# Graph attention in three layers: where vector instructions that build one-hot rows stand among the copies of gathered rows

## The chip, the cores and the metric

The kernel runs on one core of a Trainium2 chip. Five engines work side by side, each on its own instruction queue: TensorE (PE, with its weight loads shown as PEld), VectorE (DVE), ScalarE (ACT), GpSimd (POOL) and SyncE (SP, which only issues transfers here). The metric is the device time of one execution in microseconds (us), lower is better; a comparison uses the median of several runs.

## The reference

Three layers of a graph transformer over 6250 nodes of 64 values and 206250 directed edges, which are sorted by their target node. For each edge a score is formed from the target's query and the source's key plus an edge term; a softmax over the edges of each target weighs the sources' values, which are summed:

```python
q = x @ Wq + bq
kj = (x @ Wk + bk)[src] + edge_attr @ We
alpha = jnp.sum(q[dst] * kj, axis=-1) / jnp.sqrt(D)
p = jnp.exp(alpha - segment_max(alpha, dst)[dst])
w = p / segment_sum(p, dst)[dst]
agg = segment_sum((v[src] + e) * w[:, None], dst)
x = agg + x @ Ws + bs
```

ReLU follows each layer and a layer norm the first two; behind the third stand a log-softmax, the sum with the input and a last norm.

## The kernel before

The sorted edges are cut into chunks of 768 (six tiles of 128). Four chunks are a **unit**; a layer has 67 full units and a rest. The rows `x[src]` of a unit are its 24 tiles `feat`. They come in two ways.

**Gathered.** For most tiles GpSimd issues an indirect transfer of 128 rows (`gather`, line 610). Each chunk's gathers wait for a copied index tile `gate` (ScalarE, line 642), which `release` writes two units ahead of use; four `feat` buffers are in turn.

**Picked.** In layers 1 and 2 twelve tiles of a unit (three in each of its four chunks) are not gathered but picked by TensorE out of the node table `parts`, which lies in SBUF. So twelve gathers a unit are left. A pick multiplies a one-hot `hot` by parts of the table (line 1453) into the PSUM tile `ps_x`, which then holds, for each wanted row, four candidates side by side. VectorE takes the first with a copy (line 1408) and lays the other three over it under the mask `which` with three predicated copies (line 1410). The one-hot comes from `keys`, numbers that an SP transfer brings in (line 1913): for each tile depth `t` two comparisons with a constant (line 1382, 128 partitions by 512). Three depths make six such instructions for a unit; the mask `which` (line 1371) is one instruction more.

The class `Picker` drives this. `plan` gives three depths for each of two pairs of chunks; `picks` makes four steps of a unit from that: pair 0 with depths 0 and 1, pair 0 with depth 2, pair 1 with depths 0 and 1, pair 1 with depth 2. I call them the first to the fourth pick. One is made in each quarter `j` of a unit's loop, for the unit after it. `aim` hands a free one-hot buffer (there are four) to the next depth whose keys are `ready` and issues the mask and the comparisons. A buffer becomes free when the last pair that reads it has been multiplied, so two in the third pick and one in the fourth. `ready` is renewed at a unit's end, and there all six comparisons for the coming unit are issued in a row. `evacuate` issues the copies of a pick, `swap` three small ScalarE copies behind each pair.

All engines have their order fixed by the program's order (manual schedule), so an instruction that waits holds up what stands behind it on its engine.

A quarter of unit u also turns one chunk's rows with PE transposes (line 1754), which need that chunk's gathers, and ScalarE copies the result out (line 1757). In the second quarter, behind the second pick, VectorE forms the second half of the masked scores and their maximum for the unit before (lines 1781 and 1794); ScalarE's exponential follows (line 1800), and at the end of the third quarter PE transposes its result (line 1814). The weighted sums are line 1826.

In the first layer the sorting of the edges runs on VectorE and TensorE as well, and one-hots and copies are woven into it.

Of the kernel before, what the change touches and what calls it, by code (L numbers as in the profile page):

```python
# [17 lines left out]
ALU = mybir.AluOpType  # L18
# [22 lines left out]
KB = 4  # L41
# [11 lines left out]
NH = WB // KB  # L53
# [379 lines left out]
def main_path(  # L433
# [53 lines left out]
    nc = tc.nc  # L487
# [46 lines left out]
    def ps(use):  # L534
        tag = bank_of.get(use, use)
        wide = 2 if len(psum) > 1 and tag == "x" else 1
        return psum[-1].tile(
            [P, wide * 512], F32, tag=tag, name=f"ps_{tag}", bufs={"a": 2, "x": 2}.get(tag, 1)
        )
# [7 lines left out]
    def placed(layer, k):  # L547

        return k < NT and (layer > 0 or k >= U0)
# [105 lines left out]
    rank = const.tile([P, NH], F32, name="rank")  # L655
# [691 lines left out]
    class Picker:  # L1347


        def __init__(self, layer):  # L1350
            self.layer = layer
            self.room = 4 if layer else 2
            self.plan = {k: depth(picked(layer, k)) for k in range(len(batches)) if picked(layer, k)}
            self.todo = [(k, t) for k in self.plan for t in range(self.plan[k][0])]
            self.free = list(range(self.room))
            self.hots = {}
            self.which = {}
            self.quarter = 0
            self.swaps = []
            self.late = []  # L1360
            self.ready = set(keys)

        def aim(self):

            while self.free and self.todo and (self.layer, self.todo[0][0]) in self.ready:
                k, t = self.todo.pop(0)
                n = 2 * sum(t < most for most in self.plan[k]) * P
                if k not in self.which:
                    m = NP * LB
                    which = small.tile([P, m, KB], F32, name="which", bufs=2)  # L1370
                    nc.vector.tensor_tensor(
                        which,
                        kbs[:, k].rearrange("p v c -> p (v c)").unsqueeze(2).to_broadcast([P, m, KB]),
                        four[:, :KB].unsqueeze(1).to_broadcast([P, m, KB]),
                        ALU.is_equal,
                    )
                    self.which[k] = which
                at = self.free.pop(0)
                hot = stock[0].tile([P, NH, LB * P], F32R, name=f"hot{at}", bufs=1)[:, :, :n]
                first = t * LB * P  # L1380
                for h in range(NH):
                    nc.vector.tensor_scalar(  # L1382
                        hot[:, h], keys[self.layer, k][:, first : first + n], rank[:, h : h + 1], None, ALU.is_equal
                    )
                self.hots[k, t] = at, hot

        def swap(self, left=0):

# [8 lines left out]
        def evacuate(self):  # L1397

            if not self.late:
                return  # L1400
            k, pair, t, m, px, which = self.late.pop()
            found = loaded[self.layer, k][:, 2 * pair : 2 * pair + 2, t : t + m, 0]
            which = which.rearrange("p (t c) b -> p c t b", c=LB)[:, 2 * pair : 2 * pair + 2, t : t + m]
            px = px.rearrange("p t c b d -> p c t b d")

            def choose(b):
                if not b:
                    nc.vector.tensor_copy(found, px[:, :, :, 0])  # L1408
                    return
                nc.vector.copy_predicated(  # L1410
                    found,
                    which[:, :, :, b].bitcast(I32).unsqueeze(3).to_broadcast([P, 2, m, D]),
                    px[:, :, :, b],
                )
                if b == KB - 1 and t + m == self.plan[k][pair]:
                    self.swaps.append((k, pair, t + m))

            woven.extend((pair, partial(choose, b)) for b in range(KB))
            if self.layer or len(opened) > 1:
                weave(KB)  # L1420

        def flush(self):
# [14 lines left out]
        def batch(self, k):  # L1437

            for pair, t0, m in self.picks(k):
# [3 lines left out]
                self.aim()  # L1443
                bank = "x" if self.layer else "pssp"[self.quarter]
                px = ps(bank)[:, : m * 512].rearrange("p (t c b d) -> p t c b d", t=m, c=2, b=KB)
                for t in range(t0, t0 + m):
                    at, hot = self.hots[k, t]
                    for v in range(2):
# [12 lines left out]
                        self.free.append(self.hots.pop((k, t))[0])  # L1461
                self.late.append((k, pair, t0, m, px, self.which[k]))
                if self.layer:
                    due = len(self.swaps)
                    self.evacuate()
                    self.swap(len(self.swaps) - due)
                self.aim()
                yield
# [520 lines left out]
    for layer in range(L):  # L1989
# [8 lines left out]
        for u in range(NU - 2):  # L1998
# [10 lines left out]
            for j in range(LB):  # L2009
# [14 lines left out]
                    line.weights(u - 1, 1)  # L2024
                if j == 1:
                    line.begun()
                    if not layer and placed(0, u + 1):
                        line.most(u - 1, 1)
                        line.powers(u - 1)
# [39 lines left out]
                picker.flush()  # L2069
            picker.ready.update(keys)  # L2070
            picker.aim()
            for k in range(u + 2, u + 4):
                decode(layer, k)

# [134 lines left out]
```

## Time and profile before

| | |
|---|---|
| time, median of 3 runs | 4135.28 us (4134.92 to 4141.25) |
| the profiled execution | 4139.31 us, its span 4137.5 us |
| mean granted TensorE clock | 0.933 |
| busy, share of the span | PE 81%, PEld 58%, DVE 72%, ACT 57%, POOL 68% |
| gathers of layer 0 / of layers 1 and 2 | 1100 (`feat<-in_x`) / 1592 (`feat<-x,gate`) and 48 (`feat<-x,src_b`) |

In a group's row the columns are line, engine, operation, tiles, count, then busy us and mean ns of one, then the idle time of the engine just before these instructions and what ended it. A row of the timeline has start, duration, engine, line, operation, tiles, count of merged neighbours, and in brackets the idle time before. "issue" means that the engine waited for nothing that the profile shows.

### The profile page before, as it was taken

What the parts mean: (1) busy time and instruction counts of PE and PEld (TensorE: products, weight loads), DVE (VectorE), ACT (ScalarE), POOL (GpSimd) and SP (SyncE); (2) the same over time, 40 slices, a digit from 0 to 9 for tenths busy, and PEclk for the clock granted to TensorE, in tenths of its full rate; (3) what the DMA queues carried; (4) which work ended last, traced back from release to release, by engine and by line L of the source; (5) the groups of instructions that cost most, each with busy time, mean ns of one, the idle gap of its engine ahead of it and who ended that gap; (6) DMA issues with size and microseconds to landing.
All of it is one profiled execution on the core that took longest, in us unless ns stands there. A gap on an engine that the chain in (4) does not pass through costs nothing.

```text
span 4137.5 us, 105363 instructions
## 1 busy us (share of the span) xinstructions
PE 3364.6 (81%) x34183; PEld 2391.6 (58%) x34183; DVE 2977.8 (72%) x10306; ACT 2351.6 (57%) x6011; POOL 2827.9 (68%) x2774
## 2 busy tenths in 40 slices
PE   3889899999989899984778788888757878778776
PEld 1445555555555555553666666666646666666664
DVE  5677888888878888864667777777646667777775
ACT  0455565565656555563556556565635656666665
POOL 5467666666667666663777777777657777777774
PEclk9899999999999999996999999999969999999998
DMA  5667677666767666765677777777657677777774
GB/s 111 185 175 198 171 192 181 180 183 184 188 161 193 179 180 175 183 174 125 173 183 193 186 183 185 188 189 188 164 135 183 173 190 182 187 189 183 186 184 102
DMA packets 787997, 728.88 MB, mean 176 GB/s; under 512 B 487336, under 2 KB 612450, under 8 KB 787440
## 3 DMA queue, kind: packets, MB, share of 16 engines
q1 hardware_dynamic: 630436, 504.14, 47.6%
q0 software_dynamic: 88448, 90.75, 11.6%
q10 hardware_dynamic: 68556, 127.16, 8.7%
q8 instruction: 278, 4.55, 0.5%
q14 instruction: 279, 2.29, 0.2%
HBM read 562.78 MB, written 158.81 MB: 174 GB/s over the span
## 4 chain that ended last, share of the span: by engine, by line


## 5 line engine op out<-in xcount | busy, mean ns | idle before, releaser
L610 POOL DMA_INDIRECT feat<-x,gate x1592 | 1579.9, 992 | 485.4 <-issue 372.9
L610 POOL DMA_INDIRECT feat<-in_x,gate x1100 | 1175.4, 1069 | 652.6 <-ACT gate L642 323.5
L1453 PE MATMUL ps_x<-parts,hot 128*128 128x256 f32 x6336 | 941.8, 301 | 0.0
L1453 PEld LDWEIGHTS ps_x<-parts,hot 128*128 128x128 f32 x6336 | 841.8, 202 | 81.8 <-DVE feat L1410 62.5
L1757 ACT COPY featT<-ps_a 64x384 f32<-64x384 f32 x1320 | 627.1, 475 | 393.5 <-PE ps_a L1754 369.5
L1410 DVE COPY_PREDICATED feat<-which,ps_x 128x256 f32<-128x256 int32 (+1 forms) x1584 | 592.4, 374 | 54.3
L1408 DVE COPY feat<-ps_x 128x256 f32<-128x256 f32 (+1 forms) x528 | 187.7, 355 | 587.0 <-PE ps_x L1453 577.2
L1754 PE MATMUL ps_a<-ident,feat 128*128 128x128 f32 x2380 | 451.0, 289 | 176.2 <-DMA feat<-x,gate 139.7
L1101 DVE TENSOR_SCALAR hit<-ruler,pos 128x384 bf16<-128x384 f16 x1608 | 501.8, 324 | 30.3 <-PE ps_m L1121 30.2
L1754 PEld LDWEIGHTS ps_a<-ident,feat 128*128 128x128 f32 x2380 | 283.3, 144 | 385.7 <-issue 276.0
L1382 DVE TENSOR_SCALAR hot<-keys,rank 128x512 fp32r<-128x512 f16 (+1 forms) x1040 | 432.9, 482 | 9.1 <-DMA keys<-keyS 5.2
L1826 PE MATMUL ps_p<-feat,probT 128*32 128x128 f32 x6600 | 236.3, 295 | 91.4 <-ACT probT L1817 77.8
L1112 PE MATMUL ps_x<-hit,raw 128*64 128x384 bf16 x1608 | 293.8, 360 | 2.5 <-DVE hit L1101 2.2
L1112 PE MATMUL ps_x<-hit,rest 128*64 128x384 bf16 x1608 | 275.0, 338 | 0.0
L1112 PE MATMUL ps_x<-hit,end 128*64 128x384 bf16 x1608 | 274.2, 337 | 0.0
L1826 PEld LDWEIGHTS ps_p<-feat,probT 128*32 128x32 f32 x6600 | 193.6, 119 | 129.4 <-ACT probT L1817 102.9
L1767 PE MATMUL ps_s<-featT,q 128*32 128x384 f32 x1866 | 228.0, 496 | 11.6 <-DMA featT<-eaS 7.3
L1814 PE MATMUL ps_s<-ident,prob 128*128 128x128 f32 (+1 forms) x417 | 81.3, 307 | 191.6 <-ACT prob L1800 188.7
L1453 PE MATMUL ps_p<-parts,hot 128*128 128x256 f32 x992 | 163.8, 311 | 80.5 <-DVE feat L1410 73.5
L1800 ACT ACTIVATE prob<-prob,part 128x768 f32<-128x768 f32 x204 | 190.0, 931 | 68.7 <-DVE part L1794 60.1
L1453 PEld LDWEIGHTS ps_p<-parts,hot 128*128 128x128 f32 x992 | 137.1, 204 | 112.5 <-DVE feat L1410 91.8
L1833 ACT COPY part<-ps_p 128x128 f32<-128x128 f32 (+1 forms) x140 | 37.3, 267 | 244.9 <-PE ps_p L1826 239.8
(281 smaller groups left out, 5960.6 us busy)
## 6 DMA issues: line engine op xcount, KB each, us to landing
featT<-eaS SPq DMA_DIRECT2D x658, 192.0 KB
feat<-eaP SPq DMA_DIRECT2D x134, 768.0 KB
raw<-in_ea SPq DMA_DIRECT2D x536, 96.0 KB
eaS<-eT ACTq DMA_DIRECT2D x134, 384.0 KB
keys<-keyS SPq DMA_DIRECT2D x132, 384.0 KB
eaP<-feat ACTq DMA_DIRECT2D x128, 384.0 KB
shade<-maskS SPq DMA_DIRECT2D x198, 192.0 KB
fourth<-eaS SPq DMA_DIRECT2D x134, 192.0 KB
```

Source lines behind the costliest of these rows:

```text
L610: nc.gpsimd.indirect_dma_start(out=feat[:, c, t, 0], out_offset=None, in_=xts[layer][:, :], in_offset=bass.IndirectOffsetOnAxis(ap=index[: ...
L1101: nc.vector.tensor_scalar(hit, ruler, self.pos[:, at : at + 1], None, ALU.is_equal)
L1112: nc.tensor.matmul(self.px[j * D : (j + 1) * D, :HE], self.parts[2 * h + i].thirds[part][:, j, t * D : (t + 1) * D], self.hits[h, 2 * i + ...
L1382: nc.vector.tensor_scalar(hot[:, h], keys[self.layer, k][:, first : first + n], rank[:, h : h + 1], None, ALU.is_equal)
L1408: nc.vector.tensor_copy(found, px[:, :, :, 0])
L1410: nc.vector.copy_predicated(found, which[:, :, :, b].bitcast(I32).unsqueeze(3).to_broadcast([P, 2, m, D]), px[:, :, :, b],)
L1453: nc.tensor.matmul(px[:, t - t0, v].rearrange("p b d -> p (b d)"), hot[:, h, (2 * pair + v) * P : (2 * pair + v + 1) * P], those[:, i, b0 ...
L1754: nc.tensor.transpose(pt[:, t * P : (t + 1) * P], rows[:, 2 * t * D : 2 * (t + 1) * D], ident)
L1757: nc.scalar.copy(featT[:, :, h, :], pt[h * D : (h + 1) * D, : n * P].rearrange("d (i e) -> d i e", e=P))
L1767: nc.tensor.matmul(p_s[rows, :w], self.q[:, rows], self.featT[j][:, cols], start=True, stop=True)
L1800: nc.scalar.activation(self.prob[:n, : self.cols], self.prob[:n, : self.cols], AF.Exp, bias=neg, accum_out=self.part[:n, P + 1 : P + 2],)
L1826: nc.tensor.matmul(p_g[rows, :].rearrange("n (h d) -> n h d", h=2), self.probT[:, t, rows], batch[:, j, t], start=(t == 0), stop=(t == sel ...
```

## The change

In layers 1 and 2 `aim` no longer issues the two comparisons of a depth; it puts them on a list `cuts`. `cut` issues the oldest of the list. `evacuate` issues a pick's four copies and one listed comparison behind each; `batch` calls `aim` once more before `evacuate`, so that buffers which the pick has just freed are handed on at once, and issues what is left of the list behind the copies. `cut_for` issues, ahead of a pick's products, those of its own one-hots that still stand on the list. The keys count as ready in the second quarter instead of at the unit's end. Layer 0 keeps its order.

```diff
@@ aim
+                those = keys[self.layer, k][:, first : first + n]
                 for h in range(NH):
-                    nc.vector.tensor_scalar(
-                        hot[:, h], keys[self.layer, k][:, first : first + n], rank[:, h : h + 1], None, ALU.is_equal
+                    self.cuts.append(
+                        partial(nc.vector.tensor_scalar, hot[:, h], those, rank[:, h : h + 1], None, ALU.is_equal)
                     )
                 self.hots[k, t] = at, hot
+                if not self.layer:
+                    self.cut(NH)
+
+        def cut(self, n=1):
+
+            while n and self.cuts:
+                self.cuts.popleft()()
+                n -= 1
+
+        def cut_for(self, *those):
+
+            last = max(i for i, at in enumerate(self.hots) if at in those)
+            self.cut(max(0, len(self.cuts) - NH * (len(self.hots) - 1 - last)))
@@ evacuate
+            if self.layer:
+                for b in range(KB):
+                    choose(b)
+                    self.cut()
+                return
             woven.extend((pair, partial(choose, b)) for b in range(KB))
-            if self.layer or len(opened) > 1:
+            if len(opened) > 1:
                 weave(KB)
@@ batch
+                self.cut_for(*((k, t) for t in range(t0, t0 + m)))
...
                 if self.layer:
+                    self.aim()
                     due = len(self.swaps)
                     self.evacuate()
+                    self.cut(len(self.cuts))
                     self.swap(len(self.swaps) - due)
@@ the loop over a unit's quarters
                 if j == 1:
                     line.begun()
+                    if layer:
+                        picker.ready.update(keys)
...
             picker.ready.update(keys)
             picker.aim()
+            picker.cut(len(picker.cuts))
```

Only VectorE's order differs; the other four engines have the same instructions in the same order. (Lines above 1354 are numbered higher in the changed file: the comparisons are line 1394 there, the copies 1423 and 1425, the mask 1372.)

VectorE at the end of a unit in layer 2 and in the first quarter of the next, before: the third pick's copies (two depths wide), the fourth's (one depth wide), the mask, six comparisons, the first half of the masked scores, the first pick's copies.

```order
L1408 COPY feat<-ps_x 128x2x128
L1410 COPY_PREDICATED feat<-which,ps_x 128x2x128 x3
L1408 COPY feat<-ps_x 128x2x64
L1410 COPY_PREDICATED feat<-which,ps_x 128x2x64 x3
L1371 TENSOR_TENSOR which<-kbs,four 128x64
L1382 TENSOR_SCALAR hot_55809<-keys,rank 128x512 x2
L1382 TENSOR_SCALAR hot_55812<-keys,rank 128x512 x2
L1382 TENSOR_SCALAR hot_55815<-keys,rank 128x512 x2
L1781 ISA prob,most<-ps_s,shade 128x384
L1781 ISA most 128x1
L1408 COPY feat<-ps_x 128x2x128
L1410 COPY_PREDICATED feat<-which,ps_x 128x2x128 x3
```

The same place now, from the third pick's copies on:

```order
L1423 COPY feat<-ps_x 128x2x128
L1394 TENSOR_SCALAR hot_55757<-keys,rank 128x512
L1425 COPY_PREDICATED feat<-which,ps_x 128x2x128
L1394 TENSOR_SCALAR hot_55757<-keys,rank 128x512
L1425 COPY_PREDICATED feat<-which,ps_x 128x2x128
L1394 TENSOR_SCALAR hot_55758<-keys,rank 128x512
L1425 COPY_PREDICATED feat<-which,ps_x 128x2x128
L1394 TENSOR_SCALAR hot_55758<-keys,rank 128x512
L1423 COPY feat<-ps_x 128x2x64
L1425 COPY_PREDICATED feat<-which,ps_x 128x2x64 x3
L1804 ISA prob,most<-ps_s,shade 128x384
L1804 ISA most 128x1
```

Four comparisons stand behind the four copies of the third pick, and none is left at the unit's end.

The second quarter of the unit that follows, now (mask, second pick's copies, second half of the masked scores and the maximum):

```order
L1372 TENSOR_TENSOR which<-kbs,four 128x64
L1423 COPY feat<-ps_x 128x2x64
L1394 TENSOR_SCALAR hot_55953<-keys,rank 128x512
L1425 COPY_PREDICATED feat<-which,ps_x 128x2x64
L1394 TENSOR_SCALAR hot_55953<-keys,rank 128x512
L1425 COPY_PREDICATED feat<-which,ps_x 128x2x64 x2
L1804 ISA prob,most<-ps_p,shade,most 128x384
L1804 ISA most 128x1
L1817 TENSOR_SCALAR part<-most 128x1
```

The other two comparisons and the mask stand here, in the second pick and not in the fourth: the fourth buffer is free already when the keys become ready in the second quarter. The masked scores now stand behind two comparisons more.

More of the change, by code (lines that the diff above doesn't have):

```diff
@@ L1356, in __init__ @@
             self.hots = {}
+            self.cuts = deque()
             self.which = {}
```

## The prediction

> **What bounds the kernel now.** I first read how each engine is loaded in layers 1 and 2, where alone the change acts (busy time by stage; columns are stretch, length, PE, PEld, DVE, ACT, POOL, clock, transfers).
>
> ```profile
> 1950.00:2980.00 1030.00, 829.37 (x8738) 674.98 (x8737) 709.16 (x2171) 605.18 (x1565) 788.49 (x793) 0.95 0.71 182
> 3040.00:4090.00 1050.00, 820.78 (x8658) 684.89 (x8659) 719.68 (x2239) 636.05 (x1613) 802.44 (x813) 0.92 0.71 178
> ```
>
> PE looks fullest. The groups of POOL in the same two stretches say otherwise:
>
> ```profile
> L610 POOL DMA_INDIRECT feat<-x,gate x790 | 786.6, 996 | 240.9 <-issue 188.5 <-DMA feat<-x,gate 16.5 <-DVE hot L1382 6.7
> L610 POOL DMA_INDIRECT feat<-x,gate x792 | 783.3, 989 | 241.5 <-issue 181.4 <-DMA feat<-x,gate 18.9 <-ACT gate L642 7.6
> ```
>
> 786.6 + 240.9 is 1027.5 of 1030 us. The idle part is 240.9 / 790 = 0.305 us for each gather, and the timeline has this same 0.30 before every one, whatever releaser is named: POOL takes a gather, pauses 0.30, takes the next, and never waits. So POOL bounds both layers. The timeline of POOL shows the ends of these unbroken runs:
>
> ```profile
> 1922.18 1.46 POOL L610 DMA_INDIRECT feat<-x,src_b  x1 [59.04 <-PE ps_a L1512]
> 2987.56 0.94 POOL L610 DMA_INDIRECT feat<-x,gate  x1 [0.30 <-issue]
> 3034.61 1.59 POOL L610 DMA_INDIRECT feat<-x,src_b  x1 [46.10 <-PE ps_a L1512]
> 4094.62 1.03 POOL L610 DMA_INDIRECT feat<-x,gate  x1 [0.30 <-issue]
> ```
>
> Layer 1 is 1066 us of gathers and a tail of 46, layer 2 is 1061 us and a tail of 42 to the span's end at 4137.5. The number of gathers doesn't change, nor the pause. What can change is how long one takes. The view of the gather's line has minimum/median/maximum:
>
> ```profile
> L610 POOL DMA_INDIRECT feat<-x,gate x790: 941/947/2572, 1953.4 to 2979.7; - x198
> L610 POOL DMA_INDIRECT feat<-x,gate x792: 940/947/1996, 3066.0 to 4089.6; - x198
> ```
>
> Half of all are at 0.941 to 0.947, yet the means are 0.996 and 0.989. The excess over 0.945 is 0.051 x 790 + 0.044 x 792 = 75 us. Where it falls, the timeline tells:
>
> ```profile
> 2507.91 0.97 DVE L1410 COPY_PREDICATED feat<-which,ps_x 128x128 f32<-128x128 int32 x3
> 2508.78 0.22 DVE L1371 TENSOR_TENSOR which<-kbs,four 128x64 f32<-128x64 uint8 x1
> 2508.92 2.66 DVE L1382 TENSOR_SCALAR hot<-keys,rank 128x512 fp32r<-128x512 f16 x6
> 2509.67 1.25 POOL L610 DMA_INDIRECT feat<-x,gate  x1 [0.30 <-issue]
> 2511.22 1.18 POOL L610 DMA_INDIRECT feat<-x,gate  x1 [0.30 <-issue]
> 2512.70 0.94 POOL L610 DMA_INDIRECT feat<-x,gate  x1 [0.30 <-issue]
> 2465.03 1.21 DVE L1574 TENSOR_TENSOR w<-both,mm 128x1024 f32<-128x1024 f32 x1
> 2465.17 1.90 POOL L610 DMA_INDIRECT feat<-x,gate  x1 [0.30 <-issue]
> ```
>
> The two gathers that run beside the six one-hot comparisons take 1.25 and 1.18, 0.54 us too much; the next is back at 0.94. The predicated copies, which read PSUM, lengthen nothing. Over all 116 such blocks from 2050 to 2980 and 3100 to 3990 us, the timeline's rows give 0.44 us of excess for a block. With 66 units of picks in a layer, so 132 blocks, that is **58 us of the 75**: the only part of the bound that the change touches.
>
> **The change part by part.** *Removed and added.* Nothing is removed: six comparisons and one mask a unit before and after. No transfer and no other engine's instruction moves. The six comparisons leave the unit's end; four go behind the third pick's copies, two behind the second pick's.
>
> *What a comparison costs POOL there.* No row shows one standing alone in these layers, so I read the rule of the clash. In the last two rows above the gather starts 0.14 inside a long vector instruction that ends at 2466.24; its excess of 0.95 carries it to 2466.12, so it waited from its start to 0.12 before that end. Laid against the 116 blocks this holds with 0.13, and a second point shows: 0.48 us into its work a gather needs the same thing again, and a comparison that began before then, and ends later than 0.83 after the gather's own start, holds it until its end. A comparison that begins later waits itself. Blocks of six by this rule cost 0.43 and 0.44 us in the two layers, measured are 0.43 and 0.45, so I trust it. Durations for it:
>
> ```profile
> L1410 DVE COPY_PREDICATED feat<-which,ps_x 128x256 f32<-128x256 int32 x789 | 352.2, 446 | 27.0
> L1382 DVE TENSOR_SCALAR hot<-keys,rank 128x512 fp32r<-128x512 f16 x784 | 325.9, 484 | 0.0
> L1410 DVE COPY_PREDICATED feat<-which,ps_x 128x128 f32<-128x128 int32 x789 | 238.0, 302 | 27.1
> ```
>
> A comparison shows 0.48 us and in a block the next begins 0.395 after it (undisturbed blocks of six last 2.46). One at a random moment meets a gather's start in 0.48 - 0.13 - 0.07 = 0.28 us of its length (a gather that starts within its first 0.07 isn't held) and holds it 0.14 on average; with a gather every 1.25 us that is 0.28 / 1.25 x 0.14 = 0.03 us, and the second point adds under 0.01. Six alone: 0.21 us a unit. In a block it is twice that, since a gather that was held at its start meets the next comparison but one at its second point: 1.25, not 1.1. With a copy of 0.30 to 0.45 between, comparisons begin 0.53 to 0.74 apart and some of that remains. I replayed the new order by the same rule from the moments at which the second and third pick's copies begin in this trace: 0.06 us for the second pick, 0.21 for the third, 0.27 together. **The gain is 0.44 - 0.27 = 0.17 us a unit, 132 x 0.17 = 22 us.** Bounds: comparisons that meet no gather, -58 us; each of the four or so gathers now met paying what each of the two pays today (0.22), 0.88 - 0.44 = +0.44 a unit, +58 us. I take the replay, nearest to rows.
>
> The Trainium skill, page "SBUF — State Buffer", section "Who interferes with whom", says that VectorE and GpSimd share a port pair under an exclusive lock, that whichever starts first holds it for its whole instruction, and that `tensor_scalar` in its two-port mode takes it. That a comparison holds off a gather agrees; "for the whole instruction" does not hold on GpSimd's side, since the first row pair shows six comparisons done in 2.66 us (0.20 over the undisturbed 2.46) while two gathers ran.
>
> *What VectorE pays.* Three copies of 0.446 last 1.39 in a row (its row stands in the next fence), 0.03 apart, as each reads what the last wrote; but the mask begins 0.10 before the last copy's end (2508.88 against 2508.78) and a comparison 0.08 before the mask's. So a comparison between two copies starts in the copy's last 0.10 and costs 0.35 + 0.395 - 0.476 = 0.27, not 0.395. VectorE is busy 6 x 0.13 = 0.8 us a unit less. That is off the bound and earns nothing, but where the block left, up to 2.5 us come free at the unit's end.
>
> *What waits longer.* The second pick's last copy ends 2 x 0.27 = 0.54 us later, the third's 3 x 0.27 = 0.8. Behind the second stand the maximum, ScalarE's exponential and PE's transposes of it; PE waits for those already. The waits of the two stretches, and who waited for the gathers:
>
> ```profile
> PE ps_s L1814 <- ACT prob L1800: 71.2, 58, 2.8
> PE ps_s L1814 <- ACT prob L1800: 116.6, 57, 3.8
>   PE ps_a L1754: 86.4, 73
>   PE ps_a L1754: 70.6, 48
> 2502.98 1.39 DVE L1410 COPY_PREDICATED feat<-which,ps_x 128x256 f32<-128x256 int32 x3
> 2507.58 0.29 DVE L1408 COPY feat<-ps_x 128x128 f32<-128x128 f32 x1 [3.21 <-PE ps_x L1453]
> ```
>
> 0.54 x 66 = 36 us a layer more of the first kind at most. PE has 86 and 71 us a layer in which it waits for gathers, and these shrink first. Of this cover 11 us a layer goes as POOL gets faster; 75 and 60 are left against 36, so it costs nothing. Without the cover it would be the whole 36 a layer. The third pick's 0.8 us lies in VectorE's wait of 3.21 for the fourth pick.
>
> *The new wait.* The comparison in the second quarter needs the keys that SP asks for at the end of the unit before:
>
> ```profile
> 2503.99 0.41 SPq L1913 DMA_DIRECT2D keys<-keyS  x1
> 2516.99 0.28 DVE L1408 COPY feat<-ps_x 128x128 f32<-128x128 f32 x1
> ```
>
> 13 us lie between; most of those transfers land 4 to 5 us after issue by their semaphore's events. If one were late, the second pick's copies and the maximum would queue behind it. I take zero. One-hots ready earlier for PE earn nothing: PE shows no wait for `hot`.
>
> **Sum.** Span 4137.5 - 22 + 2 (PE runs closer to the bound, so the tails may begin a little later; my estimate from that thinner cover) = 4117. The profiled execution took 4139.3, 4 us above the runs' median, so 4135.3 - 20 = **4115 us**.
>
> **The rivals.** *PE becomes the bound (slower).* Place: exponential to transposes in the third quarter. If the delays of both picks reach PE in full, it is 1.34 x 66 = 88 us a layer against 75 and 60 of cover: PE then sets the pace, 86 - 88 and 71 - 88 make +2 and +17 us on today's time, and lags carried into the two tails some 5 more, 4160. It decides from 1.1 us a unit in layer 1 and 0.9 in layer 2. For it: layer 2 already waits 116.6 us there. Against: ScalarE is often not ready either, and the third pick's delay has 3.21 us of room.
>
> *Every met gather pays as now (slower).* The upper bound, 4193; against it stands the rule's agreement.
>
> *Nothing comes of it.* If the clash depends on the comparisons' total length alone, which is unchanged, excess stays 0.44: 4135. For it: 2.46 us at a random clash of 0.18 us for each us gives today's figure as well.
>
> *More than replayed.* If the copies' beginnings drift to where gathers are past both points, 0.12 a unit: 4135 - 42 = 4093. The change does what it says, by the order of instructions.
>
> *The whole-instruction lock.* If a lone comparison waits for a gather's end and then holds up the next by 0.395 - 0.305 = 0.09, six cost 0.54 a unit, +13 us: 4148. The six done in 2.66 us beside two running gathers speak against it. It is what the Trainium skill's page "SBUF — State Buffer" gives in the section named above, taken literally.
>
> **How the numbers follow.** Forecast 0.65, nothing 0.11, PE's bound 0.10, more 0.06, every gather pays 0.04, lock 0.04. The likeliest case's own range is 4104 to 4127; the range for 8 in 10 takes in nothing-comes-of-it and part of the slower cases and of the larger gain: 4097 to 4145. About 0.2% (8 us) is what can be told from no change. Faster: 0.65 x 0.94 + 0.06 = 0.67; within: 0.65 x 0.06 + 0.09 + 0.02 + 0.02 = 0.17; slower 0.16.
>
> **What would show it.** POOL's gaps in both layers stay at 0.30 (else the bound moved). Mean gather falls from 0.996 and 0.989 to about 0.98 and 0.975, its median stays. PE's wait for gathers shrinks by 15 to 45 us a layer, its wait for `prob` grows by up to 36. Comparisons begin 0.08 to 0.10 inside the copy before. Wrong would be: gaps of POOL over 0.4 us, PE waiting less than some 10 us for gathers, excess of 0.4 or more around the two picks, or VectorE waiting for keys.

## The result, and the profile after

| | before | changed |
|---|---|---|
| median, 18 runs each on one chip | 4142.55 us (4134.11 to 4149.90) | 4154.54 us (4147.06 to 4168.23) |
| the profiled execution, its span | 4139.31, 4137.5 us | 4161.44, 4159.7 us |
| granted clock of the profiled execution | 0.933 | 0.924 |
| layer 1, between the first `src_b` gathers | 1112.4 us | 1102.8 us |
| layer 2, from its first `src_b` gather to the span's end | 1102.9 us | 1119.3 us |

The ratio is 1.0031, interval 1.0022 to 1.0040: slower by 12 us, where 20 us less was forecast. The two layers did opposite things: layer 1 became 9.6 us shorter, layer 2 16.4 us longer. Layer 0, whose order is the same, ended 15.4 us later in the profiled execution.

The timeline of GpSimd (POOL) in the changed kernel has the starts from which the table is worked out, and one of the new gaps:

```profile
1937.62 1.45 POOL L610 DMA_INDIRECT feat<-x,src_b  x1 [58.99 <-PE ps_a L1535]
3040.45 1.60 POOL L610 DMA_INDIRECT feat<-x,src_b  x1 [51.03 <-PE ps_a L1535]
3877.27 0.94 POOL L610 DMA_INDIRECT feat<-x,gate  x1 [2.84 <-ACT gate L642]
4099.82 0.94 POOL L610 DMA_INDIRECT feat<-x,gate  x1 [0.30 <-issue]
```

The groups of POOL in the same two stretches as in the prediction (1950 to 2980 and 3040 to 4090 us) show shorter gathers:

```profile
L610 POOL DMA_INDIRECT feat<-x,gate x789 | 771.8, 978 | 240.5 <-issue 183.2 <-DMA feat<-x,gate 18.3 <-ACT feat L1409 7.3
L610 POOL DMA_INDIRECT feat<-x,gate x788 | 769.2, 976 | 249.8 <-issue 184.4 <-ACT gate L642 17.9 <-DMA feat<-x,gate 15.6
```

A gather takes 0.978 and 0.976 us on average, where it took 0.996 and 0.989. So GpSimd did get the gain. In layer 1 its unbroken run is 1066.3 - 1051.8 = 14.5 us shorter, and 5 us of that are lost again in the tail (46.1 to 51.0). In layer 2 the run is 1061.0 us before and 1060.3 after: what the gathers gave went into seven gaps of 0.65 to 2.84 us, 11.7 us together of which 2.1 are the usual pauses, each ended by ScalarE's `gate`. In all seven that copy stands in ScalarE's order behind an instruction of line 1557, 1592 or 1648 (they finish nodes whose edges are done) that had waited 1.7 to 3.7 us for VectorE. Before, such a delay did no harm, as `gate` is written ahead of its gathers: worked out from the starts, by 20 us on average in the last eighth of layer 2. Now it is 2.6 us there (layer 1: 21.5 and 14.1), because the loop over the units has fallen behind GpSimd. The tail grew from 41.9 to 59.0 us. In layer 2 the bound has moved to TensorE and the chain that it waits for.

TensorE's waits for the probabilities, and who waited for the gathers, in the same two stretches:

```profile
PE ps_s L1837 <- ACT prob L1823: 131.6, 62, 3.5
PE ps_s L1837 <- ACT prob L1823: 170.3, 63, 4.1
  PE ps_a L1777: 30.0, 26
  PE ps_a L1777: 37.7, 32
```

The first kind grew from 71.2 to 131.6 and from 116.6 to 170.3 us; the second fell from 86.4 to 30.0 and from 70.6 to 37.7. All of PE's idle time, worked out from its instructions over a whole layer, went from 239.3 to 238.9 us in layer 1 and from 259.7 to 270.3 in layer 2; the same 8835 matmuls of layer 2 were busy 849.0 us, not 843.2.

VectorE with one unit in the changed kernel shows the new order and its cost:

```profile
2510.40 0.29 DVE L1423 COPY feat<-ps_x 128x128 f32<-128x128 f32 x1 [0.44 <-PE ps_x L1474]
2510.61 0.48 DVE L1394 TENSOR_SCALAR hot<-keys,rank 128x512 fp32r<-128x512 f16 x1
2511.00 0.30 DVE L1425 COPY_PREDICATED feat<-which,ps_x 128x128 f32<-128x128 int32 x1
2511.20 0.48 DVE L1394 TENSOR_SCALAR hot<-keys,rank 128x512 fp32r<-128x512 f16 x1
2511.59 0.63 DVE L1425 COPY_PREDICATED feat<-which,ps_x 128x128 f32<-128x128 int32 x2
2512.13 0.61 DVE L1804 CUSTOM_DVE_ANT_0 prob<-ps_p,shade,most 128x384 f32<-128x384 f32 x1
```

A comparison begins 0.08 to 0.10 us inside the copy ahead of it, as forecast. From the second pick's first copy to the masked scores and their maximum (line 1804) it is 1.73 us here and 1.75 on average over both layers; before it was 1.20. VectorE is busy 2913.4 us where it was 2977.8, 64 us less.

### The profile page after: what moved, and what is told of

It reads as the page before. It is cut to its first block, busy times and chain, and to the rows that moved or that the text cites. A ratio compares the mean times of both kernels' runs of the same rounds, so it can differ in the third digit from the quotient of the medians.

```text
span 4159.7 us, 105361 instructions
## 1 busy us (share of the span) xinstructions
PE 3376.2 (81%) x34183; PEld 2414.9 (58%) x34183; DVE 2913.4 (70%) x10306; ACT 2355.2 (57%) x6011; POOL 2806.9 (67%) x2774
## 4 chain that ended last, share of the span: by engine, by line
## 5 line engine op out<-in xcount | busy, mean ns | idle before, releaser
L610 POOL DMA_INDIRECT feat<-x,gate x1592 | 1555.2, 977 | 494.8 <-issue 371.2
L1777 PE MATMUL ps_a<-ident,feat 128*128 128x128 f32 x2380 | 440.7, 291 | 75.2 <-DMA feat<-x,gate 41.1
L1394 DVE TENSOR_SCALAR hot<-keys,rank 128x512 fp32r<-128x512 f16 (+1 forms) x1040 | 486.5, 482 | 13.2 <-DMA keys<-keyS 9.7
L1804 DVE CUSTOM_DVE_ANT_0 prob<-ps_s,shade 128x384 f32<-128x384 f32 x204 | 113.0, 554 | 240.8 <-PE ps_s L1790 235.4
L1837 PEld LDWEIGHTS ps_s<-ident,prob 128*128 128x128 f32 (+1 forms) x417 | 49.7, 158 | 338.9 <-ACT prob L1823 335.0
```

The costliest lines, as they stand in the source:

```text
L610: nc.gpsimd.indirect_dma_start(out=feat[:, c, t, 0], out_offset=None, in_=xts[layer][:, :], in_offset=bass.IndirectOffsetOnAxis(ap=index[: ...
L1394: self.cuts.popleft()()
L1777: nc.tensor.transpose(pt[:, t * P : (t + 1) * P], rows[:, 2 * t * D : 2 * (t + 1) * D], ident)
```

## Experiments

Eighteen runs of eleven kernels, the changed one among them, were made on several chips. On the chip of the result and on chip 14 the kernel before takes about 4143 us; on chips 2, 4, 5, 8 and 13 the same kernel takes 5590 to 5645 us, and there TensorE stalls without waiting for anything that the profile shows (399 times, 401 us in layers 1 and 2 of the changed kernel on chip 4, never on the chip of the result), and GpSimd waits for it. Ratios are against the kernel before on the same chip in the same session. Two rows of the page of the changed kernel on chip 4 show what is different there:

```profile
L610 POOL DMA_INDIRECT feat<-x,gate x1592 | 1547.4, 972 | 1359.9 <-ACT gate L642 920.1
L1849 PE MATMUL ps_p<-feat,probT 128*32 128x128 f32 x6600 | 401.8, 343 | 357.4 <-issue 189.4
```

GpSimd waits 920 us for `gate`, and TensorE loses 189 us in the weighted sums alone to "issue", waiting for nothing that the profile shows. All runs but those with doubled comparisons were on such chips, so they tell what the parts cost TensorE, not what they are worth to GpSimd.

The theory is called T in the expectations: the two comparisons in the second pick stand ahead of the maximum, the exponential and TensorE's transposes, and lengthen TensorE's chain. R1 puts the cost on the four comparisons of the third pick, R2 on neither, and R3 says that a maximum put ahead of the copies holds the copies up.

**The comparisons taken out of the second pick.** The keys count as ready in the third quarter. In the first form four comparisons lie between the third pick's copies and two between the fourth's; in the second four lie in the third pick and two right behind it.

```diff
 in the quarter loop, both forms
                 if j == 2 and layer:
                     line.powers(u - 1)
+                    picker.ready.update(keys)
...
                 if j == 1:
                     line.begun()
-                    if layer:
-                        picker.ready.update(keys)
 in batch, first form only
                     self.evacuate()
-                    self.cut(len(self.cuts))
```

> The change with the keys ready only in the third quarter: the six comparisons stand behind the third and fourth pick's copies, none ahead of the maximum. Theory T (the two comparisons of the second pick delay maximum, exponential and transposes, and PE became the bound): PE's wait for prob falls from 131.6 and 170.3 us in the two stretches back to 70 to 85 and 115 to 130, POOL's mean gather stays at 0.975 to 0.985, POOL's pauses stay at 0.30, ratio to the kernel before 0.994 to 0.997. Rival R1 (the four comparisons behind the third pick's copies are the delay): ratio 1.003 to 1.008. Rival R2 (the loss has nothing to do with either place): ratio 1.002 to 1.004.

> The change with the keys ready only in the third quarter, as in e1, meant for a chip at some 4140 us. T: PE's wait for prob back to 70 to 85 and 115 to 130 us in the two stretches, POOL's pauses 0.30 throughout, mean gather 0.975 to 0.985, ratio 0.994 to 0.997. R1 (four comparisons behind the third pick): 1.003 to 1.008. R2 (neither): 1.002 to 1.004.

> The change with the keys ready only in the third quarter, a third time, in the hope of a chip on which the kernel before takes some 4140 us (the two calls before met one with 5590 us on which TensorE waits for its own instructions). There T: PE's wait for prob back to 70 to 85 and 115 to 130 us in the two stretches, POOL's pauses 0.30 throughout, ratio 0.994 to 0.997. R1: 1.003 to 1.008. R2: 1.002 to 1.004. On a chip at 5590 us: 0.994 to 0.996 again, which would tell nothing new.

> The change with the keys ready in the third quarter and all six comparisons in the third pick: four between its copies, two right behind, none in the second pick. On a chip where the kernel before takes some 4140 us: T (the second pick's two comparisons, ahead of the maximum, cost PE's chain) 0.994 to 0.998, PE's wait for prob 70 to 85 and 115 to 130 us in the two stretches; R1 (what follows the third pick is what costs) 1.003 to 1.010. On a chip where it takes 5600 us, where the change gave 0.9972 and the version with third and fourth pick 0.9939 to 0.9974: T 0.994 to 0.997, R1 0.998 to 1.003.

> All six comparisons at the third pick, nothing left out. On a chip where the kernel before takes about 4140 us theory T expects 0.994 to 0.998 of it: the gathers are as short as in the change (0.975 to 0.98 us) and the maximum follows the second pick's copies after 1.20 us as before, so TensorE's wait for the probabilities does not grow. The rival that any shift of the comparisons into a pick costs TensorE as much expects 1.002 to 1.004, as the change. On a chip where the kernel before takes about 5600 us the ratio measured there before, 0.993, comes again.

> All six comparisons at the third pick, on a chip that takes about 4140 us for the kernel before, if it is met again. Theory T, with the doubled comparisons measured at +7.5% ahead of the maximum and at no loss behind it: copies to maximum back at 1.20 us, gathers 0.975 to 0.985 us, and 0.994 to 0.998 of the kernel before, 20 to 35 us below the change. Rival (the interleaving itself costs, or the gathers' gain is worth nothing): 1.000 to 1.004.

**Comparisons in the second pick alone.** The other four stay in a row at the unit's end.

```diff
                 for b in range(KB):
                     choose(b)
-                    self.cut()
+                    if not pair:
+                        self.cut()
...
                     self.evacuate()
-                    self.cut(len(self.cuts))
+                    if not pair:
+                        self.cut(len(self.cuts))
```

> Only the second pick's two comparisons stay among copies; the other four go to the unit's end in a row. T: the maximum is as late as in the change, PE's wait for prob stays at 125 to 175 us, ratio 1.001 to 1.006. R1: the delay is gone, ratio 0.997 to 1.000. R2: 1.002 to 1.004.

> Only the second pick's two comparisons among copies, four at the unit's end in a row, as in e3. T: PE's wait for prob stays at 125 to 175 us, ratio 1.001 to 1.006. R1: 0.997 to 1.000. R2: 1.002 to 1.004.

**The change itself again.**

> The change itself once more, beside the kernel before on the same chip, since the runs e1 to e4 met a chip on which the kernel before takes 5598 us and PE, not POOL, is the bound. On a chip at some 4140 us: ratio 1.002 to 1.004; layer 1 about 10 us shorter and layer 2 about 15 us longer than in the kernel before's profile; if layer 0, whose order is the same, again differs from that profile by some 15 us, that part is not the chance of one execution.

> The change itself beside it: 1.002 to 1.004 of the kernel before, as measured; its maximum follows the second pick's copies after 1.75 us.

| | chip: ratio and interval |
|---|---|
| third and fourth pick | 4: 0.9954 (0.9937 to 0.9972); 4: 0.9939 (0.9918 to 0.9960); 13: 0.9974 (0.9955 to 0.9993) |
| all at the third pick | 8: 0.9931 (0.9910 to 0.9952); 5: 0.9965 (0.9947 to 0.9984); 2: 0.9946 (0.9927 to 0.9966) |
| the change (third and second pick) | 4: 0.9972 (0.9950 to 0.9993); 2: 0.9971 (0.9954 to 0.9988) |
| second pick alone | 4: 1.0016 (0.9998 to 1.0034); 4: 1.0013 (0.9992 to 1.0035) |

The order is that of T: two comparisons moved into the second pick alone gain nothing (1.0016 and 1.0013, both intervals take in 1), four moved into the third gain about 0.4% beside that, and with all six away from the second the ratios are lowest. R1 falls on these chips: the kernels with most work at the third pick are the fastest. (The comparisons doubled at the third pick, below, do the same on a chip of 4143 us.) The size is small. Side by side the change is 0.33% behind the first form on chip 4 and 0.25% behind the second on chip 2, and these intervals touch. Worked out from the timelines (2700 to 3900 and 4200 to 5400 us), the maximum follows the copies after 1.20 us in both forms and after 1.74 in the change. On chips 2, 4 and 8 TensorE's transposes start 7.33 to 7.36 us after the last products of the scores have begun in the two forms, and 7.68 and 7.89 in the change; on chips 5 and 13 the two forms need 7.75 and 7.78, with no run of the change beside them.

That the change is 0.3% faster on these chips and 0.3% slower on the first has another reason than the gathers, which earn nothing where GpSimd waits anyway: the six comparisons no longer stand at the unit's end, ahead of the next unit's first copies. This is argued from the order alone.

**The maximum ahead of the second pick.** In the second quarter the masked scores go ahead of the copies, in the change and, alone, in the kernel before.

```diff
                     for i in range(max(b - a, 1)):
-                        next(picking, None)
                         if not i and j == 1:
                             line.most(u - 1, 1)
+                        next(picking, None)
```

> The change with the second half of the masked scores and the maximum ahead of the second pick's copies on VectorE, no other edit. T: the maximum comes about 1.5 us earlier than in the change, PE's wait for prob falls below that of the kernel before (under 70 and 115 us), POOL is the bound again: ratio 0.994 to 0.997. R1: the third pick still holds things up, ratio 1.001 to 1.004. R2: 1.002 to 1.004.

> The change with the maximum ahead of the second pick's copies, as in e2. T: PE's wait for prob under 70 and 115 us, POOL the bound, ratio 0.994 to 0.997. R1: 1.001 to 1.004. A new rival R3, after e4 lost 0.2% where PE was the bound: the maximum ahead of the copies holds the copies up while VectorE waits for the scores, ratio 1.000 or above.

> The kernel before with the maximum ahead of the second pick's copies. T says that POOL bounds the kernel before: PE's wait for prob falls by 20 to 60 us a layer, its wait for gathers grows by as much, the time stays: ratio 0.998 to 1.001. If the wait for prob had been the bound already, ratio 0.985 to 0.992. R1 and R2: 0.998 to 1.002.

In the change: 0.9959 (0.9939 to 0.9979) and 0.9969 (0.9950 to 0.9988). In the kernel before: 1.0022 (1.0004 to 1.0040), a little above what T expected. The maximum does come early, 2.0 us after the end of the scores' last products in place of 5.0, but the exponential follows it only 3.5 to 3.6 us later, not 1.1: it waits on ScalarE, which is not ready. TensorE's transposes gain 0.5 to 0.6 us against the change and the copies behind the maximum lose, so nothing measurable is left. R3 has this much for it; putting the maximum first is no repair.

**TensorE with less to do.** To let GpSimd set the pace again on such a chip, in layers 1 and 2 the weighted sums take two tiles of six and the picks only the rounded part of the table.

```diff
-            for t in range(self.tiles):
+            few = (0, self.tiles - 1) if self.layer else range(self.tiles)
+            for t in few:
...
-                            for i in range(2):
+                            for i in range(1 if self.layer else 2):
```

> The kernel before with less for TensorE to do in layers 1 and 2: the weighted sums take only the first and the last of a unit's tiles, and the picks only the rounded part of the table, not its rest; both are left out, and the outputs are not the reference's. Vector's and GpSimd's instructions stay as they are. All theories: TensorE no longer sets the pace, GpSimd does, so the unit period in layers 1 and 2 falls from 22 us towards 16 gathers of 0.99 us and their pauses (about 15.5 to 16), and the whole is 900 to 1100 us shorter than the whole kernel before on the same chip.

> The change with the same work left out (in layers 1 and 2 the weighted sums take only the first and the last of a unit's tiles, and the picks only the rounded part of the table). Where GpSimd is the bound, the clash of gathers and comparisons is all that counts: every theory that says that TensorE's chain undid the gain (second pick's or third pick's comparisons alike) expects gathers of 0.975 to 0.98 us against 0.99 and 15 to 35 us less than the lightened kernel before (the whole of what was predicted, 22 us, or more). If the gain is lost here too, at a TensorE with time to spare, the loss is not TensorE's, and the theory falls.

> All six comparisons at the third pick (four between its copies, two right behind), with the same work left out of layers 1 and 2 (weighted sums of the first and last tile alone, picks of the rounded part alone). Theory T (the two comparisons in the second pick lengthen TensorE's chain from the second pick's copies over the maximum and the exponential to the transposes): with time to spare on TensorE the chain does not count, so this and the lightened change are within 8 us of one another. If GpSimd still waits for TensorE's gates, this one is the faster by 10 to 25 us.

Chip 5 gave 5338.64 us (5331.39 to 5342.14), 5314.28 (5292.28 to 5346.06) and 5316.44 (5315.80 to 5320.84), 4 runs each. GpSimd did not set the pace: the whole became 305 us shorter, not 900 to 1100, and GpSimd still waited 319 to 352 us a layer in gaps. The lightened change is 24 us below the lightened kernel before, within the 15 to 35 expected, but its gathers are not shorter (0.981 us against 0.979), so the gain is not theirs. The change and the all-at-the-third are 2 us apart, as T expects with time to spare on TensorE. With GpSimd still waiting and runs that spread over 54 us this decides nothing.

**The suspected cost doubled, at either place.** Four more comparisons a unit, which write again what the one before wrote. In the first kernel they stand in the second pick, ahead of the maximum, in the second in the third pick, behind it.

```diff
                     self.cuts.append(
-                        partial(nc.vector.tensor_scalar, hot[:, h], those, rank[:, h : h + 1], None, ALU.is_equal)
+                        partial(self.compare, hot[:, h], those, rank[:, h : h + 1], 3 if self.layer and self.quarter == 1 else 1)
                     )
...
+        def compare(self, to, those, r, times):
+            for _ in range(times):
+                nc.vector.tensor_scalar(to, those, r, None, ALU.is_equal)
```

The second kernel has `2 if self.layer and self.quarter == 2 else 1` there.

> The change, with each of the two comparisons in the second pick done three times over, in place (the repeats write the same values): four comparisons a unit more, 1.6 us of VectorE between the second pick's copies and the maximum. Theory T (what stands ahead of the maximum delays TensorE): the maximum follows the copies after 3.3 us in place of 1.75, TensorE's transposes come 1.2 to 1.6 us later, and 132 units make 40 us (at the rate of the 0.2 to 0.4% that two comparisons cost before) to 210 us (all of it) more than the kernel with the same repeats in the third pick. Rival (VectorE's or GpSimd's load counts, not the place): the two kernels are within 10 us of one another.

> The change, with each of the four comparisons of the third pick done twice, in place (the repeats write the same values): the same four comparisons a unit more, but behind the maximum. Theory T: copies to maximum stays at 1.75 us, the delay lies in VectorE's wait for the fourth pick, and the time is within 15 us of the change's own (0.997 of the kernel before on a chip of 5600 us, 1.003 on one of 4140, there 5 to 15 us more for gathers that clash). Rival (load, not place): as slow as the kernel with the repeats in the second pick.

These two met chip 14, where the kernel before takes 4142.94 us (4132.81 to 4152.34). Ahead of the maximum: 4458.52 us, ratio 1.0749 (1.0729 to 1.0769). Behind it: 4146.17 us, ratio 1.0005 (0.9993 to 1.0016). The same instructions in the same number, 312 us apart by place alone; VectorE is busy 3186.5 and 3158.1 us. The rival falls. In the first, TensorE waits for the exponential, and GpSimd for TensorE (waits from 2010 to 3130 us):

```profile
PE ps_s L1841 <- ACT prob L1827: 267.6, 62, 5.7
POOL feat L610 <- ACT gate L642: 174.3, 112, 3.1
```

In the second, the same views (waits and groups of POOL from 3040 to 4090 us) read like the change's, with still shorter gathers; the last row is from the timeline and starts layer 2, the span ends at 4155.0:

```profile
PE ps_s L1841 <- ACT prob L1827: 171.9, 63, 4.1
L610 POOL DMA_INDIRECT feat<-x,gate x791 | 755.7, 955 | 266.0 <-issue 187.3 <-ACT gate L642 34.0 <-DMA feat<-x,gate 14.0
3037.71 1.60 POOL L610 DMA_INDIRECT feat<-x,src_b  x1 [61.42 <-PE ps_a L1539]
```

This is the best witness for the bound in layer 2. Its gathers are 0.955 us where the change has 0.976, which over 791 is 17 us less for GpSimd, and layer 2 takes 1117.3 us where the change takes 1119.3: the waits for `gate` doubled, 17.9 to 34.0 us, and took the gain. Its chain from copies to maximum is the change's, 1.75 us. Whatever GpSimd saves from here on, TensorE's 1117 to 1119 us stand. The 0.0026 by which its ratio lies under the change's goes with layer 1, 2 us shorter, and layer 2, 2 us shorter, and beyond that with another chip; I don't read it as a gain.

What stays open: no kernel that takes the two comparisons out of the second pick, and leaves the rest, ran on a chip of 4143 us. That it would be faster than the kernel before there is T's claim and not shown.

## Why the prediction was wrong

**Right.** The rule of the clash gave the gathers: 0.98 and 0.975 forecast, 0.978 and 0.976 measured. GpSimd's run in layer 1 was to shrink by 11 us and shrank by 14.5. The 0.54 us by which the second pick's copies end later is 0.55. VectorE was to be busy 0.8 x 132 = 106 us less and is 64 us less, which is off the bound. No wait for keys appeared. The third pick's delay was free, as the doubled comparisons there show.

**The step that failed** is this: "Of this cover 11 us a layer goes as POOL gets faster; 75 and 60 are left against 36, so it costs nothing." The cover was read from a sum over the layer, without asking where in the unit TensorE waits. Of layer 2's 70.6 us, 15.5 are waits for the layer's first gathers (`feat<-x,src_b`), ahead of the stretch in which units follow one another. The waits for gathers behind it split by place like this (worked out from the timeline, 2000 to 2960 and 3100 to 4060 us): 30 us in layer 1 and 37 in layer 2 lie between the scores' second half and the transposes of the probabilities, and 45 and 14 us elsewhere. The first kind is no cover at all. These waits run beside the very chain that was made longer (copies, maximum, exponential), so when the gather comes earlier TensorE waits for the exponential instead. The two waits moved further than the prediction gave in three of four cases: for gathers by 56 and 33 us where 15 to 45 was given, for the probabilities by 60 and 54 where 36 was the most. Four rows of TensorE's timeline in layer 2 of the kernel before show one and the same wait under two names:

```profile
3750.22 0.30 PE L1754 MATMUL ps_a<-ident,feat 128*128 128x128 f32 x1 [2.46 <-DMA feat<-x,gate]
3752.91 0.84 PE L1814 MATMUL ps_s<-ident,prob 128*128 128x128 f32 x3
3767.69 0.55 PE L1814 MATMUL ps_s<-ident,prob 128*128 128x128 f32 x3 [2.07 <-ACT prob L1800]
3783.79 0.55 PE L1814 MATMUL ps_s<-ident,prob 128*128 128x128 f32 x3 [2.53 <-ACT prob L1800]
```

In the first unit 2.46 us for the gather and then nothing for the probabilities, in the third nothing for the gather and 2.53 for the probabilities. So layer 2 had at most 14 us of cover, not 60. In the sum, the 2 us for the tails was the term that failed with it: the two tails grew by 5 and 17 us.

**What the delay costs.** I cut TensorE's unit at three marks, the first products of the scores' first half, those of their second half, and the first transposes of the probabilities. The mean times between them, worked out from the starts of 65 units a layer, are these (us, before and now):

| | layer 1 | layer 2 |
|---|---|---|
| scores' second half to transposes | 6.01, 6.37 | 6.86, 7.04 |
| transposes to the next unit's scores | 5.09, 4.88 | 4.90, 4.97 |
| scores' first half to second half | 4.44, 4.18 | 3.71, 3.71 |
| a unit | 15.54, 15.42 | 15.46, 15.72 |

The transposes come 0.36 and 0.18 us later, not 0.54. The maximum does stand 0.7 us later behind the scores, but ScalarE was often late itself and takes up half of that in layer 1 and more in layer 2. In layer 1 waits for gathers vanish in the other two parts and pay for it. In layer 2 the other two parts give nothing back: 65 x 0.255 is 16.6 us, the 16.4 by which the layer grew, 11.6 of it the later transposes and 5.1 the part behind them.

Why one layer gains and the other loses shows in the last 48 units of each. There TensorE waited for gathers for 52.6 and 26.2 us before and waits 0.0 us in both layers now, so it sets its own pace. That pace is 15.36 us a unit in layer 1, where a unit took 15.51, and 15.79 in layer 2, where it took 15.43.

**The 5 us behind the transposes** are a second price of a long wait. Two units of the changed kernel in layer 2, and the granted clock (the third number from the end) of the stretch from 3528.53 us and of that from 3543.58:

```profile
3528.53 0.90 PE L1837 MATMUL ps_s<-ident,prob 128*128 128x128 f32 x3 [3.31 <-ACT prob L1823]
3529.22 0.85 PE L1777 MATMUL ps_a<-ident,feat 128*128 128x128 f32 x3
3543.58 0.55 PE L1837 MATMUL ps_s<-ident,prob 128*128 128x128 f32 x3 [2.54 <-ACT prob L1823]
3543.96 0.49 PE L1777 MATMUL ps_a<-ident,feat 128*128 128x128 f32 x3
3528.53:3531.00 2.47, 2.47 (x12) 2.47 (x13) 1.78 (x5) 2.37 (x6) 1.85 (x3) 0.50 0.68 143
3543.58:3546.00 2.42, 2.15 (x17) 1.95 (x17) 0.96 (x4) 2.33 (x6) 1.81 (x3) 1.00 1.04 288
```

After 3.31 us of waiting three transposes take 0.90 and the next three 0.85 us, at a granted clock of 0.50; after 2.54 us they take 0.55 and 0.49, at 1.00. Of the 68 units of layer 2 the slow kind stands in 9 before, in 23 after, in 26 with the comparisons doubled at the third pick and in 52 with them doubled at the second, always inside a stretch that the trace's clock records give as 0.5. Such stretches make 188.0 us of layer 2 before and 218.5 now. Between the transposes and the next scores, units that meet half a clock for over 0.5 us there and no wait for a gather take 5.0 to 5.1 us on average, the others 4.5, and the units that meet it rise from 30 to 40 of 65. The granted clock of the long stretch is 0.91, it was 0.92:

```profile
3040.00:4090.00 1050.00, 812.13 (x8455) 682.94 (x8455) 677.19 (x2198) 625.93 (x1581) 792.75 (x812) 0.91 0.70 177
```

The Trainium skill, page "TensorE: Matmul & The Clock Gate", section "Why this matters for your kernels", says that there should be no idle gaps of TensorE over some 3 us between bursts, since after one idle window it falls back to half its clock. The rows above agree, with half the clock behind 3.31 us and all of it behind 2.54. No sharp limit shows: 22 of the 23 slow ones in layer 2 now stand behind waits of 2.42 to 4.10 us, and waits of up to 3.74 us are followed by fast ones too.

**The rivals.** "PE becomes the bound (slower)" named the place, exponential to transposes in the third quarter, and had a chance of 0.10. Its price for layer 2 was +17 us, and +16.4 was measured, but that is luck: it needed both picks' delays in full, 1.34 us a unit, and measured is 0.18 us of later transposes, against a cover that was a fifth of what it assumed. For layer 1 it gave +2, where a gain of 9.6 us came. That every gather pays, the whole-instruction lock and "nothing comes of it" are out with the gathers' mean. The forecast itself was to be called wrong at POOL gaps of over 0.4 us, and in layer 2 these are what came.

**Layer 0.** The two layers together make 6.8 us of the 12 between the medians. 15.4 of the 22 us between the two profiled executions arise in layer 0, where nothing is moved, at a clock of 0.93 to 0.96 against 0.95 to 0.97. The doubled kernels' profiled executions start layer 1 late as well (1937.1 and 1945.3 us against 1922.2), and all three lie 7 to 11 us above their medians, so I take most of it for those executions. It isn't settled.

## What to carry to other kernels

Before a wait is counted as cover for a delay, look at where it lies: a wait that runs beside the chain that grows longer will only change its name. Split an engine's waits by place in the loop, and by layer, and count as cover only what stands in series with the delay. Work taken from the bound's path is best put behind the last instruction that another engine's chain needs: the same four additional comparisons a unit cost 312 us more ahead of the maximum than behind it, where they cost about nothing.

## What the hardware showed unexpectedly

**More comparisons, a fifth of the clash.** With the four comparisons of the third pick done twice, a copy and two comparisons take 1.24 us, the gather and its pause 1.25. VectorE and GpSimd fall into step (timelines of both, layer 1):

```profile
2511.62 1.00 DVE L1393 TENSOR_SCALAR hot<-keys,rank 128x512 fp32r<-128x512 f16 x2
2512.86 1.00 DVE L1393 TENSOR_SCALAR hot<-keys,rank 128x512 fp32r<-128x512 f16 x2
2514.11 1.00 DVE L1393 TENSOR_SCALAR hot<-keys,rank 128x512 fp32r<-128x512 f16 x2
2511.42 0.94 POOL L610 DMA_INDIRECT feat<-x,gate  x1 [0.30 <-issue]
2512.67 0.95 POOL L610 DMA_INDIRECT feat<-x,gate  x1 [0.30 <-issue]
2513.92 0.94 POOL L610 DMA_INDIRECT feat<-x,gate  x1 [0.30 <-ACT feat L1413]
```

The comparisons then begin 0.2 and 0.7 us into a gather, one after its start and one past its second need, and hold nothing up. Summed over 2050 to 2980 and 3100 to 3990 us, gathers beside comparisons are 51 us over 0.945 before (about 700 comparisons), 35 after (about 700) and 10 here (about 1160). So the phase decides, not the number. By the same durations two comparisons, of the six there are, behind each of the third pick's copies should have this step; that kernel was not tried.

**A repeat is dearer than a fresh comparison.** Two rows of VectorE from the kernel doubled in the second pick:

```profile
2502.73 1.69 DVE L1393 TENSOR_SCALAR hot<-keys,rank 128x512 fp32r<-128x512 f16 x3
2504.54 1.86 DVE L1393 TENSOR_SCALAR hot<-keys,rank 128x512 fp32r<-128x512 f16 x3
```

At the 0.395 us of the blocks of six, three in a row would take 0.48 + 2 x 0.395 = 1.27 us. But 1.52 is what the five of 254 such rows take that no gather runs beside, so a repeat costs 0.52 us; the mean of all is 1.64, so the clash with gathers is the smaller part. In a block of six each comparison writes another half of a one-hot, a repeat writes the same half again; that this is the reason is not shown. The maximum came about 4.0 us after the copies (median 3.97), not 3.3, and the loss against the other place was 312 us, where 210 was the most expected.

**Half the clock, 3.41 us at a time.** The clock records of the trace of the changed kernel know two values, 1.0 and 0.5. In layer 2 there are 43 stretches at 0.5; 34 of them last 3.41 us and seven 6.83, twice that. So the slowdown behind a long wait comes in portions.

**The same kernel at 4143 and at 5600 us.** On five chips TensorE's instructions come in lumps with "issue" stalls between them; VectorE's, ScalarE's and GpSimd's instructions take as long as before. The granted clock is 0.83 there and fell to 0.78 when TensorE was given less to do. The cause was not looked for.
